# Two-layer convolution/attention kernel on one core: the last slot's inverse sums on VectorE, and an order of its own for the last band

## Chip, core and metric

The kernel runs on one core of a Trainium2 chip. Times are microseconds of device time for one execution. A profiled execution gives, beside its own time, a span: from the first to the last recorded instruction.

## What is computed

The input x has shape 4 x 128 x 64 x 64. Layer 0 normalises over the 128 channels, adds a depthwise 3x3 convolution, and attends inside windows of 16 x 16 pixels: two branches, four heads of 32 channels, each pixel looking at its 5 x 5 neighbourhood. Layer 1 works on the 4096 tokens of each image: a causal linear attention, then a recurrent network whose input is normalised over all tokens of all images. Cut to what matters:

```python
# layer 0, per window of 16x16, branch b, head h
logits = einsum('nbhdij,nbhdkij->nbhkij', q, k_nb) * HD**-0.5     # 25 neighbours, zero padding outside
attn   = softmax(logits, axis=3)
o      = einsum('nbhkij,nbhdkij->nbhdij', attn, v_nb)
x      = x + (ho[:, 0] + 0.5 * ho[:, 1]) / rect                   # ho: o times Wo
# layer 1
t = t + linear_attention(ln(t))        # num / den, running sums of k v and k
Wx = ln(t) @ W.T; Wx = (Wx - mean) * rsqrt(var + eps) * gamma + beta   # mean, var over all tokens
y_t = sigmoid(Wx_t + y_{t-1} @ V.T)    # along the tokens
out = t + y
```

A neighbour outside the window counts in the softmax as a logit of zero, that is, as one in the sum. Those ones are a constant of the pixel's place, `pad_c`.

## The kernel before, in words

There are 16 bands of 16 rows (4 images of 4 bands), and each band has 4 windows, so 64 slots. One loop (line 684, `i`) runs over the slots and two more. In slot i TensorE makes the logits of window i (`logits`), the sums and weighted values of window i-1 (`weighted`, lines 379 to 418), and GpSimd multiplies the output of window i-2 by its inverse sums (`scaled`, line 425). Work of layer 1 on the band before (`behind`, made by `layer1`) and of layer 0 on the band ahead (`ahead`) is put into the gaps between; `between` takes one step of each. The order of the instructions on each compute engine is the order in which the program issues them, and `in_order` makes it binding. SP carries almost all transfers, in one queue.

**Inverse sums.** In `weighted` a matmul with ones (line 385) gives the sum over the keys for each query, as 32 equal rows for each head (`dps`). ACT copies it to `den` (line 388). SP gathers one row of each head into `dc`, 128 x 16 (line 390), so that VectorE inverts 16 columns and not 512: it adds `pad_c` (line 408), inverts (line 410) and keeps the largest and smallest sum (lines 411, 412). SP writes the inverses to DRAM, `rd` (line 414), and reads them back spread over the 32 rows of each head, `rden` (line 416). ACT has meanwhile copied the weighted values `ops` to `o_sb` (line 405), and GpSimd multiplies the two into `oT` (line 425), the band's output before the projection.

**Layer 1 of a band** works on two halves of four tiles of 128 tokens, `a` and `c`; `y` and `z` are the halves of the band before, whose last steps are still due. `output0` (line 450) projects `oT` and adds the input (line 457). `measure` takes mean and variance (lines 191, 193 on VectorE, 195, 196 on GpSimd), `norm` applies them (line 203), `turn` transposes (TensorE line 212, copied at line 474). `queries`, `keys` (line 479, exponential on ACT line 481, VectorE lines 483, 484), `values` (lines 496, 504), `turn_keys` (lines 514, 516), `scores` (lines 522, 524 into `aT`), `accumulate` (lines 539, 547) and `attend` (lines 558 to 572) are the linear attention. Then `measure` again, `keep` (transposes at line 212, copy to `rs_o` at line 577, write to `resd` in DRAM at line 578), `norm`, `turn_last` (line 582) and `product` (line 587, copied to `wx` at line 588, its statistics at line 589). The order list stands at lines 597 to 622; `layer1_end` (lines 632 to 639) does the last steps of the very last band, whose `z` is the half of 512 tokens that ends last.

**After the loop** the pools of the main part are given back and `res` takes their place: four transfers of 2 MB (line 733), two on SP's queue and two on ACT's, read `resd` back. VectorE combines the statistics (line 739). Then the recurrence: 11 steps to warm up and 32 steps (lines 783 to 808), each of which adds `res` (line 807) and writes 256 KB of output. Tiles come from pools with a fixed number of buffers; where a tile takes the place of an older one, the program waits for the older one's last reader.

Of the kernel before, what the change touches and what calls it, by code (L numbers as in the profile page):

```python
# [17 lines left out]
P = 128  # L18
# [28 lines left out]
def conv_attn_hybrid(ctx: ExitStack, tc: tile.TileContext, ins: dict, out: bass.AP):  # L47
# [150 lines left out]

    def normed(found, tiles, tag):
        pieces, mv, rs = found  # L200
        xn = tiles.tile([P, 4, P], F32, tag=tag, name=tag)
        for j, piece in enumerate(pieces):
            nc.vector.tensor_scalar(  # L203
                xn[:, j, :], piece, mv[:, j, 0:1], rs[:, j : j + 1], ALU.subtract, ALU.mult
            )
        return xn

# [170 lines left out]

    def weighted(w):

# [8 lines left out]
        dc = p2.tile([P, 16], F32, tag="dc", name="dc")  # L389
        nc.sync.dma_start(dc, den[::HD, :])  # L390
        yield
        for br, n in pieces:
            cols, _ = spans(br, n)
            for h in range(HEADS):
# [7 lines left out]
                    stop=(br, n) == pieces[-1],  # L402
                )
        o_sb = p1.tile([P, BR * WT], F32, tag="o_sb", name="o_sb")
        nc.scalar.copy(o_sb, ops)  # L405
# [5 lines left out]
        nc.vector.tensor_tensor(dmax, dmax, dc, ALU.max)  # L411
        nc.vector.tensor_tensor(dmin, dmin, dc, ALU.min)
        rd = dram4.tile([HEADS, BR * WT], F32, tag="rd", name="rd")
        nc.sync.dma_start(rd.rearrange("h (a e) -> (h a) e", e=16), rc)
# [54 lines left out]
    def norm(h):  # L469
        h.xn = normed(h.found, p3, "xn")  # L470
# [113 lines left out]
    def product(h):  # L584
# [6 lines left out]
        )  # L591

    def layer1(n, last):

# [26 lines left out]
            (turn_last, a), (attend, c, 1), (measure, c), None,  # L621
        ]
        for what in order:
            if what is None:
                yield
            elif what[1] is not None:
                what[0](*what[1:])
        halves[n] = a, c

    halves = {}  # L630

    def layer1_end(y, z):
        norm(z)
        product(y)
        yield
        keep(z)
        turn_last(z)
        yield
        product(z)

# [43 lines left out]
    for i in range(len(places) + 2):  # L684
# [11 lines left out]
        if 2 <= i:  # L696
            scaled(m, wjm, windows.pop(i - 2))
        if i < len(places) and wj == 1 and n + 2 < len(bands):
            load(n + 2)
        sums = weighted(windows[i - 1]) if 1 <= i <= len(places) else iter(())  # L700
        for gap in (1, 2):
# [9 lines left out]
        for gap in (3, 4, 5):  # L711
            next(inputs, None)
            between(i, gap)
        run(inputs)
    run(behind)
    run(layer1_end(*halves.pop(len(bands) - 1)))
    in_order()
# [782 lines left out]
```

## Time and profile before

| | us |
|---|---|
| median of 4 runs (955.11 to 961.75) | 959.01 |
| the profiled execution | 958.08 |
| its span | 956.1 |
| TensorE busy in the span | 882.4 (92%) |
| VectorE busy | 748.3 (78%) |
| ACT busy | 543.1 (57%) |
| GpSimd busy | 262.3 (27%) |

How to read it: the chain of work that ended last is followed back from the last instruction, at each step to what released it. A row of it has the start in us from the span's start, the duration, the engine (or DMA) and the tile with its line. A group of instructions has line, engine, operation, tiles and shapes, a count, then busy time and the mean ns of one, then the engine's idle time just before. In a table of stretches a row has the stretch, its length, the busy time of TensorE, of its weight loads, VectorE, ACT and GpSimd with their counts, TensorE's granted clock as a share of the full one, the busy share of the DMA engines, and GB/s. "PE" is TensorE, "DVE" VectorE, "POOL" GpSimd, "SP" the engine that only issues transfers.

### The profile page before, as it was taken

What the parts mean: (1) busy time and instruction counts of PE and PEld (TensorE: products, weight loads), DVE (VectorE), ACT (ScalarE), POOL (GpSimd) and SP (SyncE); (2) the same over time, 40 slices, a digit from 0 to 9 for tenths busy, and PEclk for the clock granted to TensorE, in tenths of its full rate; (3) what the DMA queues carried; (4) which work ended last, traced back from release to release, by engine and by line L of the source; (5) the groups of instructions that cost most, each with busy time, mean ns of one, the idle gap of its engine ahead of it and who ended that gap; (6) DMA issues with size and microseconds to landing.
All of it is one profiled execution on the core that took longest, in us unless ns stands there. A gap on an engine that the chain in (4) does not pass through costs nothing.

```text
span 956.1 us, 26560 instructions
## 1 busy us (share of the span) xinstructions
PE 882.4 (92%) x10508; PEld 656.7 (69%) x10508; DVE 748.3 (78%) x2452; ACT 543.1 (57%) x1010; POOL 262.3 (27%) x359
## 2 busy tenths in 40 slices
PE   5979999999999999999999999999999999977784
PEld 3757777777777777677677777786767778755442
DVE  6445879888897978787888879887979787667786
ACT  3555656565656565665657565656556565522553
POOL 2113131313232321413132323223141313121185
PEclk9988999999999999999999999999999999989898
DMA  4112121121212111111212121112121111100853
GB/s 123 28 36 60 47 67 39 49 59 55 58 56 63 52 51 56 60 37 55 59 48 59 58 58 58 54 54 55 48 68 36 57 34 59 33 34 32 347 207 146
DMA packets 53045, 63.46 MB, mean 66 GB/s; under 512 B 22960, under 2 KB 33840, under 8 KB 52400
## 3 DMA queue, kind: packets, MB, share of 16 engines
q1 hardware_dynamic: 51184, 56.91, 19.0%
q10 hardware_dynamic: 1728, 4.77, 1.3%
q8 instruction: 85, 1.39, 0.6%
q14 instruction: 48, 0.39, 0.1%
HBM read 35.44 MB, written 17.30 MB: 55 GB/s over the span
## 4 chain that ended last, share of the span: by engine, by line
PE 70%; DMA 11%; DVE 7%; ACT 4%; POOL 4%; issue 2%; SPq 1%; ACTq 0%; POOLq 0%; DVEq 0%
PE bank L322 9%; PE bank L450 6%; PE bank L367 6%; PE bank L212 6%; DMA rden<-rd 6%; PE bank L397 6%; PE bank L385 6%; PE bank L479 5%; PE bank L335 5%; PE bank L558 3%; PE bank L587 3%; PE bank L539 3%; PE bank L522 3%; PE bank L560 3%; DMA res<-resd 2%; PE bank L496 2%
## 5 line engine op out<-in xcount | busy, mean ns | idle before, releaser
L273 DVE SCALAR_TENSOR_TENSOR y<-ypad,cpe_w,y 128x512 f32<-128x512 f32 x240 | 190.0, 792 | 12.9 <-ACT y L271 9.3
L425 POOL TENSOR_TENSOR oT<-o_sb,rden 128x512 f32<-128x512 f32 x64 | 84.6, 1323 | 365.8 <-DMA rden<-rd 303.0
L376 ACT ACTIVATE es<-bank 128x512 f32<-128x512 f32 x256 | 132.2, 602 | 77.0 <-PE bank L367 77.0
L196 POOL TENSOR_TENSOR rs<-rs,mhalf 128x4 f32<-128x4 f32 (+2 forms) x100 | 107.1, 1071 | 8.3
L367 PEld LDWEIGHTS bank<-q,k 32*128 32x128 f32 x3072 | 98.9, 191 | 10.6 <-ACT k L330 9.6
L367 PE MATMUL bank<-q,k 32*128 32x96 f32 (+1 forms) x3072 | 97.5, 272 | 8.7 <-ACT k L330 8.7
L203 DVE TENSOR_SCALAR xn<-x,mv,rs 128x128 f32<-128x128 f32 x256 | 82.4, 383 | 21.4 <-POOL rs L196 21.4
L195 POOL TENSOR_SCALAR rs<-mv 128x4 f32<-128x4 f32 (+2 forms) x100 | 24.9, 249 | 267.3 <-DVE mv L193 175.2
L397 PEld LDWEIGHTS bank<-es,v_sb 128*32 128x32 f32 x3072 | 57.4, 111 | 30.5 <-issue 18.2
L405 ACT COPY o_sb<-bank 128x512 f32<-128x512 f32 x64 | 37.6, 587 | 70.7 <-POOL oT L425 55.8
L385 PE MATMUL bank<-es,ones 128*32 128x512 f32 x512 | 71.2, 630 | 0.0
L479 PE MATMUL bank<-xl,awT 128*128 128x512 f32 x128 | 70.1, 631 | 0.9 <-ACT xl L474 0.9
L397 PE MATMUL bank<-es,v_sb 128*32 128x96 f32 (+1 forms) x3072 | 70.7, 241 | 0.0
L450 PE MATMUL bank<-woT,oT 128*128 128x128 f32 x512 | 66.4, 285 | 3.8 <-POOL oT L425 3.8
L450 PEld LDWEIGHTS bank<-woT,oT 128*128 128x128 f32 x512 | 63.2, 198 | 7.7 <-POOL oT L425 4.9
L322 PE MATMUL bank<-y2w,wqT 128*128 128x256 f32 x256 | 66.4, 382 | 1.1 <-DVE y2w L273 1.1
L342 ACT COPY v_sb<-bank 128x512 f32<-128x512 f32 x64 | 37.6, 588 | 52.2 <-PE bank L335 51.3
L322 PE MATMUL bank<-y2w,wkT 128*128 128x256 f32 x256 | 65.8, 380 | 0.0
L335 PE MATMUL bank<-wvT,y2w 128*128 128x256 f32 x256 | 65.8, 380 | 0.0
L330 ACT COPY q<-bank 128x512 f32<-128x512 f32 x64 | 37.8, 590 | 37.6 <-PE bank L322 37.2
L191 DVE BATCH_NORM_STATS2 st<-x 128x6 f32<-128x128 f32 x256 | 55.5, 279 | 1.1
L212 PE MATMUL bank<-ident,xf 128*128 128x128 f32 x128 | 31.5, 335 | 24.6 <-DVE xf L203 20.5
(124 smaller groups left out, 1750.0 us busy)
## 6 DMA issues: line engine op xcount, KB each, us to landing
rden<-rd SPq DMA_DIRECT2D x64, 256.0 KB
v_sb<-v_sb SPq DMA_DIRECT2D x128, 64.0 KB
resd<-rs_o SPq DMA_DIRECT2D x32, 256.0 KB
out<-ot SPq DMA_DIRECT2D x32, 256.0 KB
xin<-in_xt SPq DMA_DIRECT2D x15, 512.0 KB
res<-resd SPq DMA_DIRECT2D x2, 2048.0 KB
res<-resd ACTq DMA_DIRECT2D x2, 2048.0 KB
dc<-den SPq DMA_DIRECT2D x64, 8.0 KB
```

Source lines behind the costliest of these rows:

```text
L196: nc.gpsimd.tensor_tensor(rs[:, :n], rs[:, :n], mhalf[:, :n], ALU.pow)
L212: nc.tensor.transpose(tps[:, j * P : (j + 1) * P], xn[:, j0 + j, :], ident)
L273: nc.vector.scalar_tensor_tensor(y2, src, cpe_w[:, tap : tap + 1], y2, ALU.mult, ALU.add)
L322: nc.tensor.matmul(pps[:, br * WT : (br + 1) * WT], wT[:, br * P : (br + 1) * P], y2, start=True, stop=True,)
L335: nc.tensor.matmul(vps[:, e * 256 : (e + 1) * 256], y2[:, e * P : (e + 1) * P], wvT, start=True, stop=True,)
L367: nc.tensor.matmul(sps[h][:, cols], w["k"][rows, k0 : k0 + P], w["q"][rows, cols], start=False, stop=(br, n) == pieces[-1],)
L376: nc.scalar.activation(es, sps[h], AF.Exp, scale=scale)
L385: nc.tensor.matmul(dps[rows], ones[:, :HD], w["es", h], start=True, stop=True)
L397: nc.tensor.matmul(ops[rows, cols], w["v"][:, n, c0 : c0 + HD], w["es", h][:, cols], start=(br, n) == pieces[0], stop=(br, n) == pieces[-1],)
L425: nc.gpsimd.tensor_tensor(oTs[n][:, :, :, wj * WS : (wj + 1) * WS], w["o"].rearrange("p (a r c) -> p a r c", a=BR, c=WS), w["rden"].rearra ...
L450: nc.tensor.matmul(yps[:, j * P : (j + 1) * P], oT[:, br, t], woT[:, br, :], start=br == 0, stop=br == BR - 1,)
L479: nc.tensor.matmul(zps, awT[:, m * P : (m + 1) * P], h.xl, start=True, stop=True)
```

## The change

In the last slot (`final`) the inverse is taken at full width on VectorE: `dps` plus a full-width table of the padding (`pad_f`, a new input, read once by a transfer into a buffer that is one of the `low` tiles), then in two halves of eight rows each a reciprocal and the product with `ops`, straight into `oT`. The transfers `rd` and `rden` and GpSimd's product are not issued for this slot; the gather `dc`, the small reciprocal and the largest and smallest sums stay, and so does the copy to `o_sb`. The table's transfer is issued in the slot before.

The last band has an order list of its own, with few pauses, in which `output0` comes before the older half's last steps. The last half's second measuring, normalising, transposing and product are done in two pairs of tiles (`measure_pair`, `norm_pair`, `turn_pair`, `product_pair`), the statistics of `wx` once for both, and its `keep` is put behind the last product. `layer1_end` is gone. Otherwise the program is the same; `normed` is split in two functions that issue what it issued.

```diff
@@ -196,13 +196,16 @@
         nc.gpsimd.tensor_tensor(rs[:, :n], rs[:, :n], mhalf[:, :n], ALU.pow)
         return pieces, mv, rs
 
-    def normed(found, tiles, tag):
+    def scaled_by(xn, found):
         pieces, mv, rs = found
-        xn = tiles.tile([P, 4, P], F32, tag=tag, name=tag)
         for j, piece in enumerate(pieces):
             nc.vector.tensor_scalar(
                 xn[:, j, :], piece, mv[:, j, 0:1], rs[:, j : j + 1], ALU.subtract, ALU.mult
             )
+
+    def normed(found, tiles, tag):
+        xn = tiles.tile([P, 4, P], F32, tag=tag, name=tag)
+        scaled_by(xn, found)
         return xn
 
     def turned(xn, j0, n):
@@ -376,7 +379,7 @@
             nc.scalar.activation(es, sps[h], AF.Exp, scale=scale)
             w["es", h] = es
 
-    def weighted(w):
+    def weighted(w, final):
 
 
         ops, dps = bank(), bank()
@@ -388,6 +391,10 @@
         nc.scalar.copy(den, dps)
         dc = p2.tile([P, 16], F32, tag="dc", name="dc")
         nc.sync.dma_start(dc, den[::HD, :])
+        if final:
+
+            r = p2.tile([P, BR * WT], F32, tag="low", name="low")
+            nc.vector.tensor_tensor(r, dps, padding, ALU.add)
         yield
         for br, n in pieces:
             cols, _ = spans(br, n)
@@ -401,6 +408,15 @@
                     start=(br, n) == pieces[0],
                     stop=(br, n) == pieces[-1],
                 )
+        if final:
+
+            for k in range(2):
+                rows = slice(k * WS // 2, (k + 1) * WS // 2)
+                o, by = (
+                    x.rearrange("p (a r c) -> p a r c", a=BR, c=WS)[:, :, rows] for x in (ops, r)
+                )
+                nc.vector.reciprocal(by, by)
+                nc.vector.tensor_tensor(oTs[len(bands) - 1][:, :, rows, W - WS :], o, by, ALU.mult)
         o_sb = p1.tile([P, BR * WT], F32, tag="o_sb", name="o_sb")
         nc.scalar.copy(o_sb, ops)
         yield
@@ -410,6 +426,9 @@
         nc.vector.reciprocal(rc, dc)
         nc.vector.tensor_tensor(dmax, dmax, dc, ALU.max)
         nc.vector.tensor_tensor(dmin, dmin, dc, ALU.min)
+        if final:
+            yield
+            return
         rd = dram4.tile([HEADS, BR * WT], F32, tag="rd", name="rd")
         nc.sync.dma_start(rd.rearrange("h (a e) -> (h a) e", e=16), rc)
         rden = p1.tile([P, BR * WT], F32, tag="rden", name="rden")
@@ -586,6 +605,33 @@
         wps = bank()
         nc.tensor.matmul(wps, fwT, h.xl, start=True, stop=True)
         nc.scalar.copy(wx[:, h.b, h.hb], wps.rearrange("p (k s) -> p s k", s=SEG))
+        nc.vector.bn_stats(
+            stats[:, h.b * NH + h.hb, :], wx[:, h.b, h.hb].rearrange("p s k -> p (s k)")
+        )
+
+
+
+    def measure_pair(h, e):
+        h.found = measured([h.x[:, 2 * e + i, :] for i in range(2)], 1e-5)
+        h.pairs = getattr(h, "pairs", ()) + (h.found,)
+
+    def norm_pair(h, e):
+        if e == 0:
+            h.xn = p3.tile([P, 4, P], F32, tag="xn", name="xn")
+        scaled_by(h.xn[:, 2 * e :], h.pairs[e])
+
+    def turn_pair(h, e):
+        if e == 0:
+            h.xl = p2.tile([P, 512], F32, tag="xl2", name="xl2")
+        nc.scalar.copy(h.xl[:, e * 256 : (e + 1) * 256], turned(h.xn, 2 * e, 2)[:, :256])
+
+    def product_pair(h, e):
+        wps = bank()[:, :256]
+        nc.tensor.matmul(wps, fwT, h.xl[:, e * 256 : (e + 1) * 256], start=True, stop=True)
+        ks = slice(e * HSEGS // 2, (e + 1) * HSEGS // 2)
+        nc.scalar.copy(wx[:, h.b, h.hb, :, ks], wps.rearrange("p (k s) -> p s k", s=SEG))
+
+    def statistics(h):
         nc.vector.bn_stats(
             stats[:, h.b * NH + h.hb, :], wx[:, h.b, h.hb].rearrange("p s k -> p (s k)")
         )
@@ -620,6 +666,20 @@
             (attend, c, 0), None,
             (turn_last, a), (attend, c, 1), (measure, c), None,
         ]
+        if n == len(bands) - 1:
+
+            order = [
+                (output0, a), (measure, a), (keep, z), (norm, z), None,
+                (output0, c), (measure, c), (product, y), (turn_last, z), None,
+                (norm, a), (product, z), (turn, a), (norm, c), (queries, a), (keys, a), (turn, c),
+                (values, a), (queries, c), (scores, a), (keys, c), (turn_keys, a), (values, c),
+                (accumulate, a), (turn_keys, c), (attend, a, 0), (attend, a, 1), (measure, a),
+                (scores, c), (accumulate, c), (attend, c, 0), (measure_pair, c, 0), (norm, a),
+                (attend, c, 1), (measure_pair, c, 1), (keep, a), (turn_last, a),
+                (norm_pair, c, 0), (product, a), (turn_pair, c, 0), (norm_pair, c, 1),
+                (product_pair, c, 0), (turn_pair, c, 1), (product_pair, c, 1), (keep, c),
+                (statistics, c),
+            ]
         for what in order:
             if what is None:
                 yield
@@ -628,15 +688,6 @@
         halves[n] = a, c
 
     halves = {}
-
-    def layer1_end(y, z):
-        norm(z)
-        product(y)
-        yield
-        keep(z)
-        turn_last(z)
-        yield
-        product(z)
 
 
 
@@ -694,10 +745,14 @@
                 behind = layer1(m, halves.pop(m - 1, (None, None)))
         between(i, 0)
         if 2 <= i:
-            scaled(m, wjm, windows.pop(i - 2))
+            w = windows.pop(i - 2)
+            if i - 1 < len(places):
+                scaled(m, wjm, w)
         if i < len(places) and wj == 1 and n + 2 < len(bands):
             load(n + 2)
-        sums = weighted(windows[i - 1]) if 1 <= i <= len(places) else iter(())
+        sums = iter(())
+        if 1 <= i <= len(places):
+            sums = weighted(windows[i - 1], i == len(places))
         for gap in (1, 2):
             next(sums, None)
             between(i, gap)
@@ -712,8 +767,10 @@
             next(inputs, None)
             between(i, gap)
         run(inputs)
+        if i == len(places) - 1:
+            padding = p2.tile([P, BR * WT], F32, tag="low", name="low")
+            nc.sync.dma_start(padding, ins["pad_f"].unsqueeze(1).to_broadcast([HEADS, HD, BR * WT]))
     run(behind)
-    run(layer1_end(*halves.pop(len(bands) - 1)))
     in_order()
     main.close()
 
@@ -1480,6 +1537,7 @@
         "mask_k": mask_k.astype(ml_dtypes.bfloat16),
         "mask_q": mask_q.astype(ml_dtypes.bfloat16),
         "pad_c": pad_c,
+        "pad_f": pad_c.reshape(HEADS, BR * WT),
         "band": band.astype(ml_dtypes.bfloat16),
         "pad_n": np.repeat(pad_n[:, :, None], 4, axis=2),
         "pad_top": pad_top,
```

## Prediction, made before the changed kernel ran

> **What bounds the kernel now.** The profiled execution took 958.08 us with a span of 956.1, so 1.98 us lie around the span; the median of the four runs is 959.01, 0.93 above it. I read the whole span's slices first (TensorE over 90% busy up to slice 35, then not), then the chain of work that ended last, from 830 us on, and the busy times in narrow stretches. Up to about 833 us the change moves only one DMA on SP; everything else is in the tail. The chain there:
>
> ```profile
> 835.76 0.22 DVE aT L524
> ...
> 837.21 0.25 DVE rc L410
> 838.22 0.30 DVE state L547
> 838.64 1.79 DMA rd<-rc
> 840.49 5.11 DMA rden<-rd
> 845.73 1.27 POOL oT L425
> 847.05 3.79 PE bank L450 x16
> ...
> 875.26 0.61 DVE x L572 x2
> 875.87 0.78 DVE st L191 x4
> 876.65 0.29 DVE mv L193 x3
> 877.29 1.02 POOL rs L196
> 878.33 0.36 DVE xn L203
> 878.74 1.11 PE bank L212 x4
> 879.87 0.59 ACT xl L582
> 880.51 2.09 PE bank L587 x2
> 882.91 0.38 ACTq L733
> 883.32 22.56 DMA res<-resd
> 905.97 1.13 DVE ot L807
> ...
> 947.41 1.97 DMA out<-ot
> ```
>
> Three pieces are to be seen. From 838.6 to 847.0 the last slot's inverse sums travel to DRAM and back (1.79 + 5.11) and GpSimd multiplies (1.27); only then does TensorE begin L450. From 847.05 the last band's layer 1 runs until its last attend is added to x, at 875.87. Then a serial tail of 6.8 us leads to the issue of the four `res` loads (882.66 on SP, 882.91 on ACT), and these set the rest: the recurrence waits for them at 905.97, and from there nothing is changed. So the price of the change is the shift of the `res` issue, 882.66 now.
>
> ```profile
> 840.00:844.00 4.00, 2.81 (x15) 1.62 (x15) 2.73 (x15) 1.71 (x3) 0.59 (x2) 1.00 0.14 45
> 844.00:847.05 3.05, 0.00 (x0) 0.00 (x0) 1.72 (x5) 0.05 (x1) 1.87 (x2) 0.84 0.30 114
> 847.05:852.80 5.75, 5.75 (x27) 5.75 (x28) 1.84 (x9) 0.59 (x1) 0.00 (x0) 0.50 0.00 0
> ```
>
> The second figure of a row is TensorE's busy time and the third from the end its granted clock: 3.6 us without work (843.4 to 847.05), and then 5.75 us at half clock. The wait costs twice.
>
> **The change, step by step.**
>
> 1. *Padding.* One DMA of the 256 KB broadcast form goes into SP's queue behind the `dc` transfer at 826.24. Like rden (5.11 us) it should land near 832. The add that needs it waits anyway for ACT's copy of the same bank, 832.63 to 833.22. Behind it on the queue, `rd` and `rden` of slot 62 come some 0.9 us later: GpSimd's product for slot 62 starts near 836.7 instead of 835.87, which step 2 hides; without that cover it would cost the 0.9.
>
> 2. *Inverse on VectorE.* The add (0.69, from the row of L457, same shape from PSUM) falls into a gap of 1.08 us and delays the second attend by 0.2. Measuring x then ends at 835.95. Two reciprocals of 256 elements follow, each with a product of 256. No row shows the size, so both ends:
>
> ```profile
> L410 DVE RECIPROCAL rc<-dc 128x16 f32<-128x16 f32 x64 | 16.2, 253 | 2.2
> L569 DVE RECIPROCAL rd<-rd 128x2 f32<-128x2 f32 x64 | 10.6, 166 | 2.2
> ```
>
> Sixteen elements take 253 ns and two take 166, so 6.2 ns an element: 0.166 + 254 x 0.0062 = 1.74 us each. The lower end is a plain pass of 256 elements, about 0.33 (L817: 0.29); the upper one puts all that L410 takes beyond the plain L411 of the same size (0.11) on its 16 elements, 8.9 ns each, 2.3 us. A plain operation on 16 (L820) takes 0.17 and on two (L568) 0.16, hence the slope is the reciprocal's own and I take 1.74. With 0.38 for each product (L818 and L815 show 0.41, less overlap) this is 2 x 2.1 = 4.2 us; oT is ready at 840.2 instead of 847.0. But VectorE is in order, and aT (L524), now at 835.76, stands behind: it goes to 840.2, 4.4 late. TensorE has other work until 837.1 and then none for 3.9 us. The skill's page "VectorE: DVE Perf Modes" (section "First, the fixed hardware budget") speaks of an iterated divide with a repeat count of 8; read as eight cycles an element at the 0.96 GHz of "Trainium Kernel Development and Optimization", an estimate is 2.1 us for one, and the sum would be 0.8 worse than by the rows.
>
> 3. *From aT to L450.* Now 841.14 is the end of the attends on TensorE, 5.4 after aT. Of the 0.80 that L408 takes now beside GpSimd's product 0.16 is left (its mean alone), as that product has ended by then, so the attends end near 844.9 and L450 starts there: 2.1 earlier than 847.05, not 10. The inverse's removal exposes what waited beside it.
>
> 4. *From L450 to the last attend.* First its cover is lost: normalising the band before's last half (1.02, at 844.65 now) and its statistics lay in the wait, and now stand in VectorE's way. At full clock: 16 passes of 0.11 and the latency, 2.1, so x at 847.0; add 0.72, measure 1.05, normalise z 1.04, add 0.72, measure 1.05, statistics 0.6, normalise a 1.1, i.e. 853.3; transposes, copy, two passes and exponential 2.8, so low (L483) at 856.1, against 859.49 now. From there the order is the same, 16.4 us, so the last attend ends at 872.5: **3.4 earlier at full clock**. At half clock L450 has the 3.8 of now, and the second output, the transposes and two L587 stretch too: 1.0 to 2.5 of it is lost, by where the slow stretch begins.
>
> 5. *The tail.* Now 875.87 to 882.66 is 6.8. The quarters take off: two bn_stats and two aggregates 0.5, pow on two columns 0.3 (1.01 for four, 0.85 for three, 0.56 for one), two xn 0.5, half a copy 0.2, and the matmul 1.5 (0.6 at full clock instead of 2.09 at half). They add: statistics of half a, queued ahead of the second pair on VectorE, 0.7. And `keep` is moved to the very end, which the waits written into the changed program show: both `res` queues, VectorE's aggregate and GpSimd's memsets wait for the landing of its write. Now that write is issued at 876.95, long before. So four transposes 0.44, the rest of a copy 0.6, and the landing of 256 KB are added; a write of that size lands in 1.97 in the chain's last step. Sum: 6.8 - 3.0 + 0.7 + 1.05 + 2.0 = **7.6, 0.8 longer**. At half clock here too, 1.5 to 2 more.
>
> *Behind the load.* The aggregate now comes 1.3 after the load's issue, and then at its issue, so the recurrence reaches its wait earlier and the load stays the last: 22.56 us of 8 MB.
>
> Sum: at full clock -3.4 + 0.8 = -2.6; with a half-clock stretch behind the reciprocals -1.6 to -0.1. What decides is whether 3.9 us without TensorE work halve the clock. The row says yes for 3.6 us (843.4 to 847.05), and 876.3 to 878.7, 2.5 us, was also followed by half clock from 880.2 (the row from 878.4 to 882 gives a mean of 0.75). The page "TensorE: Matmul & The Clock Gate" (section "What's actually happening") gives windows of 3.4 us that run freely: a pause of 3.9 may straddle two, with neither idle, so the rule leaves the clock open where the row says half; by it alone the sum is anything from -2.6 to -0.1. I take the slow stretch, in its middle: **-1.0 us**, thus 957.1 for this execution and 958.0 against the median. Half a per cent, 4.8 us, is about what a measurement of this kernel can tell from no change: I forecast no difference that can be told.
>
> **Rivals.**
>
> *A. The reciprocal is a plain pass* (0.33). Then oT is ready at 837.4, aT is late by 1.6, TensorE's pause is about 1 us and the clock stays full: 2.8 more than the full-clock sum, -5.4, so 953.6. For it: other operations of VectorE on 256 elements take 0.3 to 0.5. Against: the two rows above.
>
> *B. Half clock twice: slower than before.* The quarters send TensorE from one short matmul to the next, and if the clock is halved behind the reciprocals and again from the last attend on, the tail is 9.6 instead of 6.8 while the last attend comes only 0.9 earlier: +1.9, and with the reciprocal at its upper end, 2.3, +3.0, so 961 to 962. It decides from where the tail's slow stretch begins before the second transposes. For it: the clock fell to 0.5 at 880.2 in this very tail. Against: TensorE then has work in about half of that time, more than now.
>
> *C. Keep is not waited for as I read it*, or the landing is hidden: the tail would be 2 shorter, -3.0, 956.0. Against: the waits in the program. That the change does not do what it says is in step 5: the quarters shorten the feature path, but the load is behind `keep`, which they do not touch.
>
> **How the numbers follow.** Forecast 0.62, A 0.13, B 0.15, C 0.05, others 0.05. The likeliest gives 958.0. The range reaches to A's end (953.6) and takes in B's (962.0): 953.8 to 962.2. Faster by over 0.5% (below 954.2): most of A and a little of C and the others, 0.14. Slower (above 963.8): 0.06, from B with the load or the pad transfer late as well. Within: 0.80.
>
> **What would show it.** Reciprocals of 1.7 to 1.8 us; aT near 840; a TensorE pause from 837 to 841 and a clock of 0.5 in the 7 us after 842; L450's first pass near 845; low near 857 to 858; the last attend at 873 to 875; the last `rs_o` copy ahead of the `res` issue by 2.6; that issue near 881.7. I am wrong if the reciprocals take under 0.8 us, if the `res` load no longer ends the wait at the first `ot`, or if the padding lands after 833.3 and holds VectorE.

## The result, and the profile after

The changed kernel took 959.04 us in the median of 44 executions, the kernel before 957.51 in the median of 70 beside it. The ratio is 1.0017, 95% interval 1.0007 to 1.0028: **slower by 1.6 us** (0.7 to 2.7), where 1.0 us less was forecast. It is inside the range and inside the half per cent called no difference, but on the wrong side of zero. The profiled execution took 959.41 us with a span of 957.3.

One thing has to be set aside before the traces are compared. Up to the last slot the four compute engines run the same operations in the same order in both profiles, yet the last slot's denominators (the second recorded pass of each of its four matmuls of 512 columns, L385 before and L388 after) begin at 831.91 us in the profile before, at 833.51 after, and between 827.1 and 836.7 in the 18 profiles of this study, in no order of the kernels. So all times below are counted from **the start of the last slot**; what lies ahead of it is noise of a few us.

From there the changed kernel did most of what the steps said. Its chain of work that ended last, in order of time, first around the reciprocals:

```profile
834.85 0.69 DVE low L397
...
837.51 1.65 DVE low L418
...
839.67 1.67 DVE low L418
...
841.79 0.60 DVE aT L543
```

The padding is there in time (the add, L397, starts when ACT's copy ends). Two reciprocals stand between the measuring of x and aT, and aT comes 8.2 us behind the start of the slot instead of 3.8. TensorE pauses for 3.80 us and then has one stretch of half clock (a row: the stretch, TensorE's busy time, and third from the end its granted clock):

```profile
838.65:842.45 3.80, 0.00 (x1) 0.01 (x1) 3.66 (x6) 0.55 (x2) 2.46 (x3) 1.00 0.02 3
842.45:846.06 3.61, 3.44 (x15) 3.01 (x16) 3.45 (x19) 0.85 (x3) 0.00 (x0) 0.53 0.19 73
```

The group of the reciprocals, with the mean duration in ns behind the busy time:

```profile
L418 DVE RECIPROCAL low<-low 128x256 f32<-128x256 f32 x2 | 3.5, 1731 | 0.0
```

Further on in the same chain, from the last half's products to the recurrence:

```profile
878.55 0.70 PE bank L630 x2
879.25 0.45 PE bank L215 x4
...
879.77 0.59 ACT rs_o L596
...
880.38 2.03 DMA resd<-rs_o
...
882.95 22.73 DMA res<-resd
...
905.78 0.99 DVE ot L864
906.77 0.47 DVE bank L813
...
907.38 0.65 PE bank L857
```

As predicted, the last keep's copy and the landing of its write (2.03) stand alone ahead of the `res` load. The load is issued 49.04 us behind the start of the slot, against 50.75 before: 1.7 us were gained here, more than the 1.0 that was taken. But the last output is added only 0.3 us earlier, 114.8 behind the start of the slot against 115.2. The gain is lost behind the load, in the part of which the prediction said that nothing changes. The last line shows the place: TensorE's first pass there takes 0.65 us, where the same pass took 0.38 at 900.81, before the pause. These are the same three stretches of both kernels, before the pause, in it and behind it; the kernel before, then the changed one:

```profile
902.60:906.00 3.40, 3.40 (x12) 1.60 (x12) 0.90 (x3) 2.25 (x6) 2.01 (x3) 1.00 0.39 164
906.00:907.70 1.70, 0.03 (x2) 0.04 (x1) 1.70 (x3) 0.21 (x1) 0.94 (x1) 1.00 0.00 0
907.70:911.10 3.40, 3.37 (x12) 1.75 (x12) 3.24 (x9) 2.06 (x6) 0.87 (x1) 1.00 0.61 234
```

```profile
900.00:903.97 3.97, 3.81 (x14) 1.83 (x13) 1.27 (x3) 2.69 (x7) 0.00 (x0) 1.00 0.93 396
903.97:907.38 3.41, 0.00 (x1) 0.03 (x1) 1.60 (x3) 0.21 (x1) 1.74 (x2) 1.00 0.02 7
907.38:910.91 3.53, 3.53 (x9) 2.32 (x10) 3.38 (x10) 1.32 (x4) 2.57 (x4) 0.52 0.58 225
```

TensorE runs out of work when the recurrence has used up its three `ys` buffers, and goes on when the first `ot` (the addition that needs the load) is done. Before, it runs out at 906.03, just as the first `ot` begins (905.97), and stands still for 1.67 us. After, it runs out at 903.97, 1.8 us ahead of the first `ot` (905.78), and stands still for 3.41 us, since the aggregate no longer comes 1.3 us behind the load's issue (52.06 against 50.75) but with it (49.12 against 49.04). The longer pause is followed by 3.4 us at half clock, just as the recurrence, a chain from matmul to sigmoid to matmul, starts again: 9 passes in 3.53 us where the kernel before does 12 in 3.40.

### The profile page after: what moved, and what is told of

It is laid out like the page before. It is cut to its first block, busy times and chain, and to the rows that moved or that the text cites. A ratio compares the mean times of both kernels' runs of the same rounds, so it can differ in the third digit from the quotient of the medians.

```text
span 957.3 us, 26567 instructions
## 1 busy us (share of the span) xinstructions
PE 880.9 (92%) x10510; PEld 657.2 (69%) x10510; DVE 751.8 (79%) x2457; ACT 541.8 (57%) x1012; POOL 262.5 (27%) x360
## 3 DMA queue, kind: packets, MB, share of 16 engines
q10 hardware_dynamic: 1728, 4.77, 1.3%
## 4 chain that ended last, share of the span: by engine, by line
PE 68%; DMA 11%; DVE 10%; ACT 5%; POOL 2%; issue 2%; SPq 1%; ACTq 0%; DVEq 0%; POOLq 0%
PE bank L325 9%; DMA rden<-rd 6%; PE bank L469 6%; PE bank L215 6%; PE bank L370 6%; PE bank L498 5%; PE bank L388 5%; PE bank L404 5%; PE bank L338 5%; PE bank L577 3%; PE bank L606 3%; PE bank L558 3%; PE bank L541 3%; PE bank L579 2%; DMA res<-resd 2%; PE bank L857 2%
## 5 line engine op out<-in xcount | busy, mean ns | idle before, releaser
L196 POOL TENSOR_TENSOR rs<-rs,mhalf 128x4 f32<-128x4 f32 (+3 forms) x101 | 107.5, 1064 | 8.4
L195 POOL TENSOR_SCALAR rs<-mv 128x4 f32<-128x4 f32 (+3 forms) x101 | 25.2, 249 | 260.7 <-DVE mv L193 170.2
L388 PE MATMUL bank<-es,ones 128*32 128x512 f32 x512 | 71.7, 633 | 0.0
L469 PE MATMUL bank<-woT,oT 128*128 128x128 f32 x512 | 63.9, 278 | 0.3 <-POOL oT L444 0.3
L469 PEld LDWEIGHTS bank<-woT,oT 128*128 128x128 f32 x512 | 60.8, 192 | 3.4 <-POOL oT L444 0.8
L577 PE MATMUL bank<-v,aT 128*128 128x129 f32 x256 | 52.7, 290 | 4.8 <-DVE aT L543 4.8
```

Source lines behind the costliest of these rows:

```text
L196: nc.gpsimd.tensor_tensor(rs[:, :n], rs[:, :n], mhalf[:, :n], ALU.pow)
L388: nc.tensor.matmul(dps[rows], ones[:, :HD], w["es", h], start=True, stop=True)
L469: nc.tensor.matmul(yps[:, j * P : (j + 1) * P], oT[:, br, t], woT[:, br, :], start=br == 0, stop=br == BR - 1,)
```

## The experiments

Theory **A (pause)**: the longer pause at the first `ot` halves the clock and eats the gain. Its rivals (the letters from here on are those of the experiments, not those of the prediction's rivals): **B**, the loss lies ahead of the load or ahead of the last slot; **C**, the exposed landing of the last keep eats it; and **D**, which came up when the first four runs were read: what lies around the span (device time less span) has a value of its own in each kernel, 2.75 us in the changed one against 2.2; the reason supposed was that the program's last instructions are loaded in blocks.

The time of one kernel varies from one execution to the next (standard deviations of 1.4 to 3.6 us), so 12 executions leave an error of half a us to one us in the mean. The profiles, counted from the start of the last slot, tell far more than the times. The numbers to which the texts below come back, one row for each profile; "sixth ys" is the start of step six's sigmoid behind the first `ot`, by which the price of the pause can be read. The last column but one counts VectorE's whole list, with a second program that is jumped over; of those that ran, the profiles show 2623 before, 2627 after, 2621 in e3 and 2628 in e4 and e5, the same steps apart:

| kernel | res issue | pause of TensorE | sixth ys | last ot - first ot | VectorE's instructions | around the span (mean) |
|---|---|---|---|---|---|---|
| before | 50.75 | 1.67 | 4.15 | 41.09 | 5949 | 2.24 (134 executions) |
| after | 49.04 | 3.41 | 5.36 | 42.54 | 5953 | 2.75 (46) |
| e1_fill | 48.99 | filled | 4.04 | 40.22 | 5953 | 2.68 |
| e2_keep_early | 45.94 | 1.47 | 3.93 | 41.17 | 5952 | 2.49 |
| e3_order_only | 51.78 | 2.94 | 4.89 | 41.08 | 5947 | 1.78 |
| e4_inverse_only | 50.64 | 1.79 | 3.93 | 41.17 | 5954 | 1.41 |
| e5_after_dve1 | 49.05 | 3.40 | 5.33 | 43.18 | 5954 | 1.44 |
| e6_before_dve4 | 50.72 | 1.75 | 3.76 | 39.93 | 5953 | 2.72 |
| e8_late_keep | 47.77 | 2.29 | 4.79 | 41.39 | 5952 | 2.61 |
| e9_after_fewer | 52.26 | 3.73 | 5.48 | 41.96 | 5948 | 1.92 |
| e10_keep_fewer | 47.80 | 1.90 | 3.93 | 43.77 | 5947 | 1.76 |
| e11_states_keep_fewer | 48.66 | 2.48 | 4.81 | 41.18 | 5947 | 1.77 |
| e12_after_fill_fewer | 48.93 | filled | 4.03 | 39.99 | 5948 | 1.96 |
| e13_after_again | 49.10 | 3.43 | 5.35 | 41.14 | 5953 | 2.70 |
| e14_fill_again | 52.20 | filled | 4.11 | 40.15 | 5953 | 2.58 |
| e15_before_fill | 50.15 | filled | 4.20 | 44.59 | 5949 | 2.08 |
| e16_fill_keep_fewer | 46.42 | filled | 4.77 | 40.77 | 5947 | 1.78 |

### e1_fill: the pause filled

```
         last[g] = y
+    if s == 2:
+        for _ in range(8):
+            fill = ps_m.tile([P, 512], F32, tag="bank", name="bank")
+            nc.tensor.matmul(fill[:, :GC], fvT, last[1], start=True, stop=True)
     ot = ring.tile(...)
```

> The changed kernel with eight matmuls of 256 columns on TensorE (into a spare bank, their result unused) behind the recurrence's third step, where TensorE waits for the res load: 3.4 us of work, 8 x 0.43. Theory A (pause): in the changed kernel this pause is 3.41 us instead of 1.67, the clock is halved for 3.4 us right behind it, and the recurrence, which is a chain from there on, loses about 1.0 us. With the pause filled the granted clock stays at 1.0 from 904 to 914 and the time is about 1.0 us below the changed kernel, near 958.0. Theory B (the loss lies ahead of the load: the profiled execution was already 1.6 us late when the last slot began): the time stays at that of the changed kernel, 959.0, whatever the clock does here. Theory C (the landing of the last keep's write, 2.0 us, eats the gain): also 959.0.

Measured: 957.80 us, ratio to before 0.9998 (0.9970 to 1.0026). The stretch of the filler and the one behind it:

```profile
905.40:908.70 3.30, 3.30 (x17) 2.62 (x15) 1.56 (x3) 0.16 (x1) 1.70 (x2) 1.00 0.02 7
908.70:912.10 3.40, 3.40 (x13) 1.74 (x12) 3.35 (x10) 2.12 (x6) 2.16 (x3) 1.00 0.61 234
```

The clock stays at 1.0, 13 passes are done where the changed kernel did 9, and the sixth ys comes 1.3 us earlier behind the first `ot`. That is A's mechanism, at a little more than A's price (1.0). The time agrees with A, but its interval takes in the changed kernel too; e13 and e14 were made for that.

### e2_keep_early: the last keep ahead of half a's product

```
-    (norm_pair, c, 0), (product, a), (turn_pair, c, 0), (norm_pair, c, 1),
-    (product_pair, c, 0), (turn_pair, c, 1), (product_pair, c, 1), (keep, c),
+    (norm_pair, c, 0), (keep, c), (product, a), (turn_pair, c, 0), (norm_pair, c, 1),
+    (product_pair, c, 0), (turn_pair, c, 1), (product_pair, c, 1),
```

> The changed kernel with the last half's keep moved ahead of the last half a's product, so that its write lands beside the quarters. Theory C: the res load is issued 2.2 us earlier against the start of the last slot, near 55.8 us behind it instead of 58, and the time falls by 2.2, to 956.8. Theory A: the aggregate moves by only 1.2, as it waited for the landing too, so TensorE's pause before the first ot becomes about 2.4 us instead of 3.4; if that keeps the clock up, another 1.0 is gained: 955.8. Theory B: 959.0 less the 2.2, with half clock ahead of the load in some executions.

Measured: 957.15 us, ratio 0.9985 (0.9955 to 1.0015). (The 58 and 55.8 us of that text were counted from a wrong start, by 9.0 us; from the last slot's start they are 49.0 and 46.8.) In its chain the load now hangs on the last product's copy, no landing in between:

```profile
878.24 0.71 PE bank L630 x2
...
878.98 0.38 ACT wx L632
879.36 0.17 ACTq L790
...
879.56 22.61 DMA res<-resd
```

The issue is 3.1 us earlier than in the changed kernel (45.94 against 49.04), more than the 2.2 expected, and the aggregate stands 1.1 behind it again, so the pause is 1.47 and no half clock follows (sixth ys 3.93). So the landing is a real price, as the prediction had it in its sum; it does not explain why the sum failed.

### e3_order_only and e4_inverse_only: one half of the change each

e3 keeps the transfers for the last slot and takes only the order and the quarters; e4 takes only the inverse:

```
e3:  sums = weighted(windows[i - 1], False)          # and scaled() in every slot
e4:  order of before for every band, layer1_end() behind it
```

> The kernel before, its transfers for the inverse sums kept in the last slot, with the changed order and quarters of the last band alone (the first output behind one more step, as oT comes from GpSimd). Theory A and C: the quarters and the late keep give a tail of 7.6 us instead of 6.8, the earlier part as before, so 0 to +0.8 us against the kernel before. If the loss of the changed kernel is in the order, this shows +1.5 to +2.5. Theory B (something ahead of the last slot): exactly as before, as neither the padding input nor its transfer is there.

> The kernel before, its order of the last band and its whole last half kept, with the inverse sums of the last slot on VectorE alone. Theory A: the res load and the aggregate move together, the pause before the first ot stays near 1.7 us, and the recurrence keeps its full clock; what the inverse saves is kept, 1.5 to 3 us below the kernel before. If the inverse itself is the loss (late aT, TensorE pause of 3.8 us): 0 to +1.5. Theory B (the padding input costs time ahead of the last slot): 1 us of the gain is missing, and the profile is late where the last slot begins.

Measured: e3 957.61 us, ratio 0.9991 (0.9970 to 1.0011); e4 957.74, 0.9998 (0.9977 to 1.0018). Neither half alone is measured slower than the kernel before, as the whole is, though their intervals overlap the whole's; nor does the inverse alone give the 1.5 to 3 us: its load is issued at 50.64, only 0.1 earlier. oT is ready at 8.3 us in e4 instead of 15.1, but the first output begins at 15.43, 0.3 later than before: aT is late, the attends end at 14.3, and in the order of before the band before's last keep, its normalising and product come ahead of the first output. The inverse's gain needs the new order, which puts the first output right behind the attends. In e3 the pause is 2.94, as the order by itself puts the aggregate level with the load (51.91 against 51.78), and half clock follows. In the same two runs the time around the span was 1.78 and 1.41, each within 0.3 us in all 12 executions, where before has 2.24 and after 2.75: this brought up D.

### e5_after_dve1 and e6_before_dve4: a few instructions more on VectorE

```
+    more = sp.tile([P, 1], F32, name="more")
+    for _ in range(1):          # e6: range(4), in the kernel before
+        nc.vector.memset(more, 0.0)
```

> The changed kernel with one memset of one column more on VectorE, in the wait for the res load, where it costs nothing. Its first use is a second look at the changed kernel's end: theory A says that the pause of TensorE before the first ot is again 3.0 to 3.5 us, the clock 0.5 for one stretch behind it, and last ot minus first ot 42 to 42.6 us against 41.1 in the kernel before. From the start of the last slot to the first ot it should be 72.3 again, against 74.1. Its second use is what lies around the span: 2.75 us in the mean of 46 executions of the changed kernel against 2.17 in 35 of the one before, 1.78 in the one with the order alone and 1.41 in the one with the inverse alone. Theory D: this is the loading of the program's last instructions, whose place in the blocks that are loaded depends on how many instructions each engine has. By D the one memset brings VectorE to the number of the kernel with the inverse alone, and the time around the span falls to about 1.4, with VectorE's last event 1.2 late inside the span; if D is wrong it stays near 2.75.

> The kernel before with four memsets of one column more on VectorE, in the wait for the res load. A second look at the end of the kernel before: by theory A a pause of 1.5 to 1.9 us and last ot minus first ot near 41.1; first ot 74.1 behind the start of the last slot. Theory D: VectorE now has as many instructions as in the changed kernel, and the time around the span rises from 2.17 to about 2.75; if D is wrong it stays.

Measured: e5 960.72 us, ratio 1.0023 (0.9998 to 1.0047); e6 959.79, 0.9989 (0.9967 to 1.0010). As second looks, the pause was 3.40 with half clock behind it in e5 and 1.75 without in e6, and the first `ot` came at 72.3 and 74.1, all as expected; last `ot` minus first `ot` was not (43.18 where 42 to 42.6 was expected, and 39.93 where 41.1 was). D's part came true. For D: one memset took the time around the span from 2.75 to 1.44, with VectorE's very last event late (the span ends 11.1 us behind the last `ot` instead of 9.0), and four memsets in the kernel before took it from 2.24 to 2.72. The table shows one curve over all kernels: 1.76 to 1.78 us at 5947 instructions, 1.92 to 1.96 at 5948, 2.08 to 2.24 at 5949, 2.49 to 2.61 at 5952, 2.58 to 2.75 at 5953, then a jump into the span at 5954. The four instructions more that the change gives VectorE cost 0.5 us at the end of the program, whatever they do.

### e7_before_short_warmup: the pause made longer in the kernel before

```
-    for s in range(SEG - WARM, SEG):
+    for s in range(SEG - WARM + 2, SEG):
```

> The kernel before with two of the eleven warm-up steps of the recurrence left out, so its first state is a little less settled and the outputs a little different; the rest is the same. The recurrence then reaches its wait 2.35 us earlier, while the load is where it was. Theory A: TensorE's pause grows from 1.7 to about 4.0 us, the clock is 0.5 for one stretch behind it, last ot minus first ot rises from 41.1 to about 42, and the time rises by about 1 us although work was taken out. If the pause is harmless: no difference, since the load is what the recurrence waits for.

The time, 6757.1 us (ratio 7.04, 7.02 to 7.05), says nothing on the question: the first program ends by testing how settled the recurrence was, and with two warm-up steps fewer it hands over to a second, general program, which then runs too. The profile of the first part can be read: the pause was 5.23 us (the load took 1.4 longer than before), the clock was 0.5 for 6.8 us from 909.4, the sixth ys came at 4.86 instead of 4.15 or 3.76 and the last `ot` 41.76 behind the first. The direction is A's; the price is 0.7 to 1.1 by the sixth ys.

### e8_late_keep: reciprocals behind the band before's last states

The reciprocals and products are called behind the step that makes the states and normalises half a, instead of ahead of aT; keep as in e2.

> The changed kernel with the early keep of the second experiment, and with the reciprocals and products put behind the band before's last states on VectorE, so that aT is no longer held up by them. aT should start near 3.8 us behind the start of the last slot instead of 8.2, the attends of that half with it, and L450's counterpart about 2 us earlier than in the changed kernel, near 11 us behind the start of the slot instead of 13.2. Then the res load is issued another 2 us earlier, 44 us behind the start of the slot instead of 45.9 with the early keep alone and 49.0 in the changed kernel. Theory A: the pause before the first ot stays near 1.5 us, so the gain is kept: about 2 us below the early keep, 954 to 955. If a pause of TensorE while the reciprocals run halves the clock again, half of the 2 us goes.

Measured: 956.75 us, ratio 0.9971 (0.9950 to 0.9992). The mechanism expected failed: aT was at 3.9 as hoped, but the reciprocals started only at 10.1 (the normalising ahead of them waits for GpSimd's power, and that for GpSimd's product of slot 62), so the first output began at 12.5, not 11, and the load was issued at 47.8, not 44. The issue is 3.0 ahead of the kernel before, but 1.8 behind that of the early keep alone (45.94 in e2), so the gain is not the later reciprocals'; the pause was 2.29, and half clock followed.

### e9_after_fewer to e12: without the two costs

Five memsets of the second program, which is jumped over, go from VectorE to GpSimd: nothing that runs is different, VectorE's list is five shorter. e9 has this alone, e10 with the early keep, e11 with the early keep and the reciprocals ahead of the normalising, e12 with the filler.

```
 def general(...):
-    nc.vector.memset(ones, 1.0)          # and four more
+    nc.gpsimd.memset(ones, 1.0)
```

> The changed kernel with five memsets of its second program (general, which is jumped over) given to GpSimd instead of VectorE: VectorE's list is 5 shorter, nothing that runs differs. Theory D (the end of the program is loaded by blocks, and what lies around the span goes with VectorE's number of instructions: 1.78 us at 5947, 2.2 at 5949, 2.5 at 5952, 2.7 at 5953): 2.0 us here at 5948, so about 0.7 below the changed kernel, the span as in the changed kernel. If D is wrong: 2.75. Theory A: the pause before the first ot is 3.4 us again, ys of the sixth step comes 5.3 us behind the first ot instead of 4.0.

> The early keep of the second experiment with the same five memsets moved, VectorE at 5947 instructions. Theory A: pause near 1.5 us, no half clock behind it, ys of the sixth step 3.9 us behind the first ot; theory D: 1.8 us around the span. Both: res load 46 us behind the start of the last slot, and 0.7 us below the second experiment's kernel, 955.5, which is 3 us below both kernels.

> As the tenth experiment, and the reciprocals and products put behind aT and the four states of that half, but ahead of the normalising that waits for GpSimd (the eighth put them behind that, and lost). aT near 3.9 us behind the start of the last slot instead of 8.2, oT near 10.8 instead of 8.3, the attend's matmuls in between; the first output from 12 instead of 13.2, so the res load about 1 us earlier than with the early keep alone, 45 us behind the start of the slot; half of it gone if the clock halves later and longer.

> The changed kernel with both of the found costs taken away: TensorE's pause before the first ot filled as in the first experiment, and VectorE's list shorter by five. Theories A and D together: ys of the sixth step 4.0 us behind the first ot instead of 5.35 (1.3 us), and 2.0 us around the span instead of 2.75: 2 us or a little more below the changed kernel, so 957.0 where that has 959.1, and 1 us or more below the kernel before. If either is not what holds the time, less.

Measured: e9 956.03 us, ratio 1.0001 (0.9977 to 1.0025); **e10 950.90, 0.9952 (0.9927 to 0.9977)**; e11 954.12, 1.0003 (0.9983 to 1.0024); e12 955.84, 1.0002 (0.9974 to 1.0030). D held four times more: 1.92, 1.76, 1.77 and 1.96 us around the span. e10 is the kernel that beats both, by 4.0 us here; its profiled execution was the slowest of its twelve (955.75). There the load was issued at 47.80, not at the 46 expected, as the half clock behind the reciprocals lasted 6.8 us and took in the first output; and the recurrence took 43.77, as TensorE stopped for 2.09 us at 926.4 and half clock followed from 929.0. e11 lost, like e8, as the reciprocals began at 8.35 and the first output at 15.8. e12 did not come out below e9, against the expectation; its profile did (sixth ys 4.03 against 5.48). And e9 showed something else: its load was issued at 52.26, 3.2 later than in the changed kernel, though the program is the same there. Its stretches in the last band, 3.4 us each and in step with the clock's changes:

```profile
863.30:866.70 3.40, 2.44 (x22) 2.25 (x22) 3.15 (x17) 0.00 (x0) 1.20 (x2) 1.00 0.00 0
866.70:870.10 3.40, 2.03 (x13) 1.33 (x12) 3.33 (x17) 1.17 (x2) 0.89 (x2) 1.00 0.21 77
870.10:873.50 3.40, 2.88 (x6) 1.14 (x6) 1.78 (x8) 0.86 (x2) 0.90 (x2) 0.50 0.00 0
873.50:876.90 3.40, 2.94 (x10) 1.90 (x9) 0.53 (x2) 1.12 (x3) 0.00 (x0) 0.50 0.00 0
```

And the same part of the changed kernel's profile:

```profile
870.00:873.40 3.40, 2.70 (x22) 2.38 (x22) 3.15 (x16) 0.58 (x1) 1.16 (x3) 1.00 0.00 0
873.40:876.80 3.40, 2.00 (x8) 0.85 (x7) 2.50 (x13) 1.45 (x3) 1.23 (x3) 1.00 0.21 77
876.80:880.20 3.40, 2.42 (x10) 1.44 (x11) 1.41 (x4) 1.55 (x4) 0.00 (x0) 1.00 0.00 0
```

TensorE is busy in 60% of the second stretch of e9 and the clock falls behind it; it is busy in 59% of the middle one here and the clock holds. Once halved, it stayed so in e9 until 887, though the next two stretches were 85% and 86% busy. That is rival B of the prediction (half clock twice), in 2 of the 7 profiles with this tail (e9 and e14), at 3.2 us each. Of these, 1.1 (e9) and 1.7 (e14) are already there at the last attend: in both, the first half clock, behind the reciprocals, lasted 6.8 us instead of 3.4 and took in the first output.

### e13_after_again to e16: is the pause in the times?

e13 is the changed kernel, e14 is e1, e15 the kernel before with four fillers, e16 e10 with the filler.

> The changed kernel once more, as the partner of the next run on the same chip and as a fourth look at its end. Theory A: pause 3.0 to 3.7 us, clock 0.5 behind it, ys of the sixth step 5.3 to 5.5 us behind the first ot. Theory D: 2.75 us around the span. The res load 49.0 us behind the start of the last slot, unless the clock is halved in the tail as it was in the ninth run (52.3).

> The changed kernel with the pause filled, as in the first experiment. Theory A: ys of the sixth step 4.0 us behind the first ot, and in the times 1.3 to 2 us below the run of the changed kernel beside it. If the pause does not matter for the time: the same as the changed kernel.

> The kernel before with four of the same matmuls (1.7 us) in its pause of 1.67 us. Theory A: this pause never halved the clock (ys of the sixth step 4.15 and 3.76 us behind the first ot), so the fill brings nothing: 3.8 to 4.2 again, the time that of the kernel before within its error. If filling helps by itself, for another reason than the clock: 1 us or more below the kernel before.

> The early keep with the pause filled and VectorE's list shorter by five: every cost that was found taken away. The early keep alone left a pause of 1.5 to 1.9 us without half clock, so the fill brings nothing on top by theory A, and costs up to 1 us if the eight matmuls (3.4 us) last beyond the landing of the load. Expected: ys of the sixth step 4.0 to 4.9 us behind the first ot, 1.8 us around the span, and the time near that of the tenth run, 0.995 of the kernel before.

Measured: e13 960.10 us, ratio 1.0027 (1.0005 to 1.0049); e14 956.72, 1.0003 (0.9983 to 1.0023); e15 956.70, 0.9997 (0.9975 to 1.0019); e16 954.85, 0.9982 (0.9961 to 1.0003). On one chip, the filled kernel's mean is 2.3 us below the unfilled one's (956.93 against 959.23, 12 executions each; 95% interval 0.4 to 4.2), although its profiled execution had the half clock in the tail. The other such pair on one chip, e12 against e9, shows 0.2 us the other way, with an error of 1.2; the two together give 1.4 us, give or take 1.5. So the times agree with A's price of 1.3, but the proof of it is in the profiles. The clock says the same: from the mean clock of each execution, TensorE spent 47.9 us at half clock in the changed kernel (58 executions) and 42.3 in the filled one (24), but 43.5 in e9 and 44.3 in e12. In the kernel before the same filler brought nothing (0.1 us), as A says: its pause did not halve the clock in either profile. (The 44.59 us of e15's profile are a separate thing: from 927 us on VectorE's `ot` ran beside GpSimd's in each step and took 883 ns instead of 293.) e16 gained nothing on e10, and its ratio missed the 0.995 expected; its sixth ys (4.77) fits that: the filler ended at 901.8, 2.6 us behind the start of the first `ot` (899.2), and so outlasted the landing of the load. On its chip it is still 4.7 us below the changed kernel (954.54 against 959.23 in the mean), as e10 is 4.0 below e9 on another.

## Why the prediction was wrong, step by step

1. *Padding*: right. It landed in time; the add took 0.69 as costed.
2. *Inverse on VectorE*: right. 1.72 and 1.74 us for a reciprocal (1.74 predicted), 0.43 for a product (0.38), aT 4.4 later (4.4), TensorE's pause 3.8 (3.9). The plain-pass rival A is dead, and the 2.1 of the iterated divide, which the prediction estimated from the Trainium skill's page "VectorE: DVE Perf Modes", section "First, the fixed hardware budget", was 0.4 too long.
3. *From aT to the first output*: right. 13.15 us behind the start of the slot against 15.14, so 2.0 earlier (2.1).
4. *To the last attend*: the order of work right, the price of half clock not. The last attend came 2.9 earlier, where the step said 3.4 at full clock and took off 1.0 to 2.5 for half clock. One stretch of half clock lay behind the pause (842.65 to 846.06), not the 7 us named as a sign, and it ended as the first output began (846.66), so it cost about 0.5. In e9 and e14 it lasted 6.8 us and cost 1.1 and 1.7 more. So both outcomes occur, 2.9 and about 1.5.
5. *The tail*: right in kind. 7.97 us against 6.79, so 1.2 longer (0.8), with keep's landing, 2.03, at its end. Steps 4 and 5 together make the 1.7 gained at the load in this profile.
6. *Behind the load*: **the step that failed**: "the aggregate now comes 1.3 after the load's issue, and then at its issue, so the recurrence reaches its wait earlier and the load stays the last". All of that came true, and it was priced at nothing. The earlier arrival doubles TensorE's pause, and the row that the prediction had quoted for the other pause (3.6 us, then half clock) applied here as well. The price by the sixth ys is 1.4 us (mean 5.38 of four profiles with a pause of 3.4 to 3.7, against 3.94 of five with 1.9 or less; 4.79 to 4.89 with 2.3 to 2.9). That the five short pauses went without half clock was in part luck: the stretch of 3.41 us that held most of the pause was 57 to 61% busy in four of them, where half clock can follow (last section).

   By the last `ot` the price can't be read so well: 42.2 in the mean of the same four, 40.5 in the two profiles of the kernel before and 40.1 in the three of the changed kernel filled, but 41.17 in e2 and e4, 43.77 in e10, all without half clock here, and 41.14 in e13 with it. One reason is a second stop of TensorE, in mid-recurrence near 919 to 931, of 0.9 to 2.2 us in 12 of the 17 profiles. In after, e5 and e10 the stretch of 3.41 us with this stop was 39 to 46% busy, and half clock followed; in the other nine it was 55% or more, and none did. As e10's pause was short, this second half clock is not the work of the longer pause. A block of 16 KB of instructions is fetched within 5 us ahead of this stop's end; that the fetch makes the stop is not shown.
7. *Not in the sum*: 0.5 us around the span, since VectorE has four instructions more (e5, e6, e9 to e12). The prediction took the 1.98 us around the span as fixed, a term put at nothing without a reason.
8. *Rival B* had 0.15. Its half clock in the tail occurs in 2 of 7 profiles of this tail, which in the mean takes 0.9 of the 1.7 us gained at the load.

The sum of the means: 0.9 earlier at the first `ot` (73.2 of after, e5, e9 and e13 against 74.1 of before and e6), 1.4 later by the sixth ys, 0.5 around the span: +1.0; with the 1.7 of the last `ot` in place of the 1.4, +1.3. Measured are +1.6 (0.7 to 2.7). So the mechanism of the forecast up to the load stands. That the mean there, 0.9, is so near the 1.0 taken is luck: it is made of three profiles 1.7 to 1.8 earlier and one, with rival B, 1.7 later. The gain was turned into a new wait, and the end of the program took the rest. None of the three signs by which the prediction said it would be wrong came true: all of them lie ahead of the load's landing, and the loss lies behind it.

## What to carry to other kernels

When the transfer that ends a phase is issued earlier, ask what the engines do that wait for it: if they arrive earlier too, the wait grows, and here half clock came with it. Eight matmuls into a spare bank kept the clock up and brought the time back to that of the kernel before, no further. Put the last dependent transfer of a phase ahead of what doesn't need it, so that its landing lies beside work: against the changed kernel the early keep won 3.1 us at the issue (e2), and with five instructions fewer on VectorE it was 4.0 us faster than the kernel before (e10). And where effects are near 1 us, count from an event that both programs share, and look at what lies around the span before a difference is put down to the path.

## What the runs showed of the hardware that was not expected

- **The clock follows the busy share of stretches of 3.41 us, not idleness alone.** The 17 profiles (all but e7) were cut into stretches of 3.41 us that line up with the recorded changes of the clock, and the share in which TensorE had a matmul was taken for each, in whole percent. From 50 us on, at full clock, a stretch with 51% or less was followed by half clock in 77 of 77 cases, one of 52 to 62% in 40 of 119, one of 63% or more in none of 4086. (Near 45 us, in the program's first moments, four stretches of 45 to 50% were not followed by it.) At half clock, a stretch under 88% busy never brought the full clock back (61 cases); with 88% or more it came back in 117 of 136 cases, and in all 78 from 100 us on. The Trainium skill's page "TensorE: Matmul & The Clock Gate", section "What's actually happening", speaks of half clock after an idle window and gives the free-running window of 3.4 us; the window's length agrees with the 3.41 us here, but a window that was 60% busy was enough in e9.
- **The number of instructions of one engine moves the end of the program**: 1.76 to 1.78 us around the span at 5947 on VectorE, 2.75 at 5953, and at 5954 1.4 with the span 1.8 to 2.1 longer behind the last `ot` (10.8 and 11.1 us in e4 and e5, against 9.0 after and 9.1 before). In all profiles up to 5948 the last 8 KB packet of instructions is fetched inside the span, in all from 5949 on behind it (at 957.95 before, with the span's end at 956.12). That the count decides is shown by e5 and e6, which add nothing else; that the fetch is what it acts through is inferred from this.
